# Two token-routing Mixtures of a four-layer macaron block: first choice taken from the logits, weights without shares, counts of tiles by one scan, counts of batches added on TensorE, fewer steps from rank to slot

## The chip, the cores and the metric

The kernel runs on one core of a Trainium2 chip. The metric is the device time of one execution in microseconds (us), of which several runs are taken; the median counts. The engines are TensorE (PE), VectorE (DVE), ScalarE (ACT), GpSimd (POOL) and SyncE (SP), whose queue issues most DMAs.

## The reference, cut to what matters

The input x holds 4 batches of 512 tokens of width 128, in f32. Four layers follow one another. Each is "macaron": x + half a feed-forward of norm(x), then x + attention of norm(x), then x + half the same feed-forward again. Layer 0's feed-forward is a mixture of 8 experts with one choice per token and a capacity of 320 rows per expert; layer 3's is one with two choices and a capacity of 512. Layers 1 and 2 have other forms (gated sums over all experts), which the change doesn't touch. The two mixtures, cut:

```
# layer 0: one choice
probs = softmax(tokens @ gate.T)
mask = one_hot(argmax(probs))
ranks = cumsum(mask, axis=0) - 1          # how many tokens before it chose the same expert
keep = (ranks < 320) * mask
y[t] = probs[t, e] * expert_e(row ranks[t] of e)     for kept tokens, else 0

# layer 3: two choices
scores = softmax(x @ wg)
gates, idx = top_k(scores, 2);  gates = gates / sum(gates)
m = one_hot of all first choices, then of all second choices
loc = cumsum(m, axis=0) - 1 at the chosen expert
valid = loc < 512
y[t] = sum over its two choices of gates * valid * expert(row loc)
```

An expert is relu(row @ w1 + b1) @ w2 + b2 with a middle width of 512. The cumulative sums run over all 2048 tokens, so a batch's ranks need the counts of all batches before it.

## The kernel before, in words

Tokens lie on the 128 partitions; a batch is four tiles of 128 tokens. The class `Mixture` is made four times: f00 and f01 (layer 0's two halves, k = 1) and f30 and f31 (layer 3's, k = 2). It has these parts.

`empty` and `clear` write zeros into the DRAM buffers. `tokens` (L283 to L403) routes one or two batches; it is a generator, and each `yield` gives the caller room to put other work in between. It makes the column `spare` (L303, the row past the end that a dropped token is sent to), norms (L145), transposes and the logits on PE (L322, into PSUM). The softmax (L224 to L236) takes the maximum of the logits (L227), subtracts it (L229), has ACT take exp (L230), and then sums (L233), takes the reciprocal (L234) and multiplies (L235). `route` (L205 to L216) finds the first largest of 8: maximum (L208), equality (L210), times a falling rank (L211), maximum (L213), and equality to it, which is the mask (L216). With two choices `without` (L221) takes the first one out and `route` runs again. The weights are `counts` (L339 for one choice, L346 to L349 for two). Then come the sums: `pre` holds, for every tile, how many tokens of one partition in the tiles before it chose each expert. Its first row is the running count of all earlier batches, copied in at L357, and one addition per tile follows (L359). Two matmuls make a rank of it: the masks against a strictly triangular `before` (L368), and `pre` against `ones` (L369), both summed in PSUM. From the rank DVE makes `kept` (L372), the row `at` counted from the expert's first row, or downward from its last for the second choice (L374 to L377), `slot` (L379), `keep` (L381), and with `spare` (L382, L383) the row `to` as an integer (L385). POOL copies the weights beside the normed tokens (L392) and sends each tile with an indirect DMA to its rows in DRAM (L395), one DMA for each tile and choice. At the end of the last batch PE also sums the total counts (L413), which DVE uses for the rows never written (L415, L417).

`experts` (L405) loads the sorted rows of an expert (`d_f`, on SP, L426), transposes them (`dT_f`, L442), computes h (L466) and o (L501), and scatters y back by an indirect DMA (L489). `combine` (L511) reads the results back and adds them to x.

Four places call `tokens`:

- Start: f00's four batches, two rounds apart (`skewed(choices, 2)`), in a part whose order the framework plans. Around them stand the loads of layer 0's expert weights, `prep_table` (L943: `rev` loads on SP; L948: `turned` matmuls, which make the bias table of layer 0's attention) and the first weights of that attention (L137, L140: raw_wqkvT, raw_ow0T).
- Layer 0's attention: f01's `tokens` are passed as what is done `after` each batch. That function runs in an order written by hand (`manual_schedule` for PE, DVE, ACT and POOL): `tokens` with `fine=True` goes on by one yield in each slot. The last batch's routing comes after the attention has ended, a tail with nothing beside it.
- The chain of layers 1 and 2: f30's `tokens` follow the last half feed-forward of layer 2: the first pair of batches in one call (G = 8 tiles) whose dispatch is held back by `later=4`, the second pair as two calls of one batch. Here only POOL's order is as written; the framework plans the others.
- Layer 3's attention: f31's `tokens`, as in layer 0, with a tail for the last batch.

[...] The lines that the prediction uses elsewhere: L127 and L129 are the copies from PSUM by DVE or ACT, L154 the aggregate of the norm, L157 POOL's first step of the norm, L180 transposes, L587, L672, L678 and L722 the scores, maxima and sums of layer 3's attention, L1275 and L1278 the gated products of layer 2's feed-forward (`gb_f`, `y_f`), L1307 the scan of layer 2's attention, L960 the addition of a row to x by POOL.

Of the kernel before, what the change touches and what calls it, by code (L numbers as in the profile page):

```python
# [41 lines left out]
def kernel(ctx: ExitStack, tc: tile.TileContext, a: dict, out: bass.AP):  # L42
# [25 lines left out]
    for b in range(NB):  # L68
# [13 lines left out]
    before = const([P, P], "before")  # L82
    nc.gpsimd.affine_select(
        out=before, in_=ones, pattern=[[1, P]], compare_op=ALU.is_gt, fill=0.0, base=0, channel_multiplier=-1
    )
    mhalf = const([P, 2 * NT], "mhalf")
# [118 lines left out]
    def route(pool, src, g, tag, mask=None):  # L205

        mx = pool.tile([P, g], FP, name=f"mx_{tag}", tag=f"mx_{tag}")
        nc.vector.tensor_reduce(mx, src, AX.X, ALU.max)  # L208
# [14 lines left out]

    def softmax(pool, lg, g, tag):  # L224

        mx = pool.tile([P, g], FP, name=f"smx_{tag}", tag=f"smx_{tag}")
        nc.vector.tensor_reduce(mx, lg, AX.X, ALU.max)  # L227
        pr = pool.tile([P, g, E], FP, name=f"pr_{tag}", tag=f"pr_{tag}")
        nc.vector.tensor_tensor(pr, lg, bc(mx, [P, g, E]), ALU.subtract)  # L229
        nc.scalar.activation(pr, pr, AF.Exp)  # L230
        yield
        sm = pool.tile([P, g], FP, name=f"sm_{tag}", tag=f"sm_{tag}")
        nc.vector.tensor_reduce(sm, pr, AX.X, ALU.add)  # L233
        nc.vector.reciprocal(sm, sm)  # L234
        nc.vector.tensor_tensor(pr, pr, bc(sm, [P, g, E]), ALU.mult)  # L235
        return pr  # L236
# [4 lines left out]
    class Mixture:  # L241
# [7 lines left out]
        def __init__(self, tag, cap, k):  # L249
# [9 lines left out]
            self.cum = None  # L259

# [22 lines left out]
        def tokens(self, bs, wT, on="vector", pool=None, fine=False, later=0):  # L283
# [8 lines left out]
            for n, b in zip(ns, bs):  # L292
# [8 lines left out]

            spare = pool.tile([P, k, G], FP, name=f"spare_{tag}", tag=f"spare{k}{G}")
            nc.gpsimd.tensor_scalar(  # L303
                spare, bc_mid(tok_id[:, i0 : i0 + G], [P, k, G]), float(self.rows), None, ALU.add
            )
# [28 lines left out]
            pr = yield from softmax(pool, plg[:, : G * E].rearrange("p (g e) -> p g e", e=E), G, f"r{G}")  # L334
            masks = tile("masks", [P, k, G, E])
            _, best = route(pool, pr, G, f"r0{G}", masks[:, 0])
            counts = tile("counts", [P, k, G])
            if k == 1:
                nc.vector.tensor_scalar(counts[:, 0], best, 0.5, None, ALU.mult)  # L339
            else:  # L340
                if fine:
                    yield
                rest = without(pool, pr, masks[:, 0], G, -4.0, f"r{G}")
# [6 lines left out]
            if fine:  # L350
                yield
# [1183 lines left out]
```

## Time and profile before

| what | value |
|---|---|
| runs, median (lowest to highest) | 1565.0 us (1563.73 to 1570.41), 3 runs |
| profiled execution, its own time | 1562.17 us |
| its span, first to last instruction | 1560.5 us |
| mean granted TensorE clock | 0.893 |
| busy: PE, DVE, ACT, POOL | 81%, 55%, 46%, 42% |
| PE busy in layer 0's attention with what is woven in (118 to 380 us) | 229.15 of 262 us |
| PE busy in layer 3's attention (1125 to 1433 us) | 291.09 of 308 us |
| indirect DMAs of the dispatch (L395) | 96, 983 ns each on POOL |

The span is that of one execution, taken by the hardware profiler; times on the page are us from its start, and the execution took 1.67 us more than the span. A line of the page names the source line of the kernel, the engine, the operation, the tile written and those read, with partitions and elements per partition. In a view in order of time, the number in brackets is how long the engine sat idle before the instruction, and what ended that. Shares of busy time are means over stages that have different limits.

### The profile page before, as it was taken

How to read it: one execution, taken by the hardware profiler on the slowest of the kernel's cores; microseconds unless marked ns; L12 is line 12 of the kernel's file. 1: busy time of each engine (PE TensorE's matmuls, PEld its weight loads, DVE VectorE, ACT ScalarE, POOL GpSimd, SP SyncE). 2: the span in 40 equal slices, each digit the busy share in tenths (PEclk: the TensorE clock that was granted, in tenths of full speed). 3: DMA queues.
4: the chain of work that ended last, by engine and by line, in shares of the span. 5: the costliest groups of instructions: out<-in, count | busy, mean ns of one | idle time of the engine just before them, and what ended most of it. 6: DMA issues, size and time to landing. Idle time of an engine off the chain costs nothing. (4 is left out here: it accounts for less than half of the span.)

```text
span 1560.5 us, 28691 instructions
## 1 busy us (share of the span) xinstructions
PE 1264.9 (81%) x10523; PEld 821.3 (53%) x10523; DVE 864.1 (55%) x2947; ACT 712.9 (46%) x1487; POOL 655.7 (42%) x789
## 2 busy tenths in 40 slices
PE   4777998995969688989988676718779999998394
PEld 3455676773756455766756655616533343333273
DVE  5335676773325365766556455515367787774343
ACT  1234876871443165768643322203325655564041
POOL 3455767872520176777501111273632214212253
PEclk9997999996979888999999778758979999999597
DMA  7420240002515474442033302214204000000223
GB/s 231 129 57 8 77 164 12 9 13 64 148 35 109 126 226 123 136 123 69 2 78 116 135 0 109 114 50 114 64 21 171 14 3 13 12 5 15 75 79 105
DMA packets 103092, 123.12 MB, mean 79 GB/s; under 512 B 9404, under 2 KB 74152, under 8 KB 100904
## 3 DMA queue, kind: packets, MB, share of 16 engines
q1 hardware_dynamic: 96296, 108.07, 23.2%
q0 software_dynamic: 6656, 13.22, 2.6%
q8 instruction: 84, 1.38, 0.4%
q14 instruction: 56, 0.46, 0.1%
HBM read 79.27 MB, written 41.98 MB: 78 GB/s over the span
## 5 line engine op out<-in xcount | busy, mean ns | idle before, releaser
L605 POOL TENSOR_SCALAR sc_a<-sc_a,top_a 128x128 f32<-128x128 f32 (+3 forms) x256 | 275.4, 1091 | 112.1 <-DVE top_a L604 72.2
L587 PE MATMUL s_a<-k_a,q_a 32*128 32x512 f32 (+3 forms) x1536 | 267.1, 549 | 17.9 <-DMA k_a<-fac_a 14.2
L692 ACT ACTIVATE w_a<-t_a 128x512 f32<-128x512 f32 x256 | 140.4, 595 | 119.7 <-PE t_a L587 94.8
L628 PE MATMUL t_a<-ident,sc_a 128*128 128x128 f32 x1280 | 172.3, 282 | 6.0 <-DVE top_a L608 5.6
L489 POOL DMA_INDIRECT res_f<-y_f,back_f x112 | 109.7, 980 | 141.8 <-ACT y_f L488 101.3
L587 PE MATMUL t_a<-ql_a,k_a 32*128 32x512 f32 x512 | 168.8, 643 | 0.5 <-DVE low_a__12599 L672 0.2
L628 PEld LDWEIGHTS t_a<-ident,sc_a 128*128 128x128 f32 x1280 | 145.1, 144 | 36.8 <-issue 13.8
L617 ACT ACTIVATE sc_a<-sc_a,top_a 128x128 f32<-128x128 f32 (+3 forms) x256 | 135.0, 577 | 23.8 <-DVE top_a L608 23.6
L587 PEld LDWEIGHTS s_a<-k_a,q_a 32*128 32x128 f32 x1536 | 93.7, 188 | 88.9 <-issue 43.1
L637 ACT ACTIVATE w_a<-t_a 128x256 f32<-128x256 f32 (+2 forms) x192 | 94.2, 526 | 64.2 <-PE t_a L628 63.7
L395 POOL DMA_INDIRECT disp_f<-n_f,to_f x96 | 94.3, 983 | 66.8 <-issue 58.8
L501 PE MATMUL o_f<-w_l,h_f 128*128 128x128 f32 (+1 forms) x896 | 113.0, 279 | 3.8 <-DVE o_f L483 3.3
L501 PEld LDWEIGHTS o_f<-w_l,h_f 128*128 128x128 f32 (+1 forms) x896 | 103.0, 184 | 14.7 <-DVE o_f L483 6.0
L466 PE MATMUL h_f<-dT_f,w_l 128*128 128x320 f32 (+1 forms) x256 | 107.8, 559 | 2.8 <-ACT dT_f L444 2.8
L157 POOL TENSOR_SCALAR rs_f<-mv_f 128x4 f32<-128x4 f32 (+1 forms) x23 | 6.5, 281 | 233.4 <-DVE mv_f L154 232.7
L650 PE MATMUL acc_a<-w_a,vpad 128*32 128x128 f32 x2560 | 98.4, 280 | 0.6 <-DVE top_a L604 0.6
L639 ACT COPY w_a<-t_a 128x256 f32<-128x256 f32 (+2 forms) x192 | 93.7, 528 | 6.7 <-PE t_a L628 6.5
L672 DVE TENSOR_REDUCE low_a__12599<-s_a 128x1 f32<-128x512 f32 x128 | 82.1, 685 | 26.3 <-PE t_a L587 18.5
L608 DVE CUSTOM_DVE_ANT_0 sc_a<-s_a,future 128x128 f32<-128x128 f32 (+3 forms) x128 | 62.3, 487 | 57.2 <-PE s_a L587 44.2
L672 DVE TENSOR_REDUCE low_a__12597<-s_a 128x1 f32<-128x512 f32 x128 | 81.3, 683 | 20.5 <-PE t_a L587 15.1
L608 DVE CUSTOM_DVE_ANT_0 sc_a<-s_a,table 128x128 f32<-128x128 f32 (+3 forms) x128 | 62.4, 487 | 53.0 <-PE s_a L587 52.5
L488 ACT ACTIVATE y_f<-o_f,d_f 128x128 f32<-128x128 f32 (+1 forms) x112 | 38.8, 394 | 105.9 <-DVE o_f L483 102.3
(337 smaller groups left out, 2260.8 us busy)
## 6 DMA issues: line engine op xcount, KB each, us to landing
gb_f<-rows_f SPq DMA_DIRECT2D x16, 1024.0 KB
fac_a<-fac_a_sb SPq DMA_DIRECT2D x36, 256.0 KB
disp_f<-zeros_f SPq DMA_DIRECT2D x4, 2080.0 KB
d_f<-disp_f SPq DMA_DIRECT2D x32, 260.0 KB
w_l<-in_L_ffn_w_dram SPq DMA_DIRECT2D x16, 512.0 KB
cb_f<-rows_f SPq DMA_DIRECT2D x16, 512.0 KB
q_a<-fac_a SPq DMA_DIRECT2D x32, 256.0 KB
k_a<-fac_a SPq DMA_DIRECT2D x32, 256.0 KB
```

The lines of the kernel that those rows point to most:

```text
L395: nc.gpsimd.indirect_dma_start(out=self.to[c][i0 + t][:, :], out_offset=bass.IndirectOffsetOnAxis(ap=to[:, c, t : t + 1], axis=0), in_=ns[ ...
L466: nc.tensor.matmul(ps[u][:, :cap], w1[:, e, (c + u) * P : (c + u + 1) * P], dT, start=True, stop=True)
L489: nc.gpsimd.indirect_dma_start(out=self.back[e * per + s][:, :], out_offset=bass.IndirectOffsetOnAxis(ap=back[:m, s : s + 1], axis=0), in_ ...
L501: nc.tensor.matmul(po[:m, s, :], h[:, c, s * P : s * P + m], w2[:, e, c, :], start=(c == 0), stop=(c == NC - 1),)
L587: nc.tensor.matmul(ps[:, n0:n1], q[r : r + SLOT, i * P : (i + 1) * P], k[r : r + SLOT, n0:n1], start=True, stop=True)
L605: nc.gpsimd.tensor_scalar(sc, sc, top, None, ALU.subtract)
L608: nc.vector.tensor_tensor_reduce(sc, banks[r][:, :n], more, -1.0, HUGE, ALU.add, ALU.min, top)
L617: nc.scalar.activation(sc, sc, AF.Exp, bias=top, scale=-1.0)
L628: nc.tensor.transpose(ps[:, x * n + j * P : x * n + (j + 1) * P], st["sc", u, i, r0 + x][:, j * P : (j + 1) * P], ident,)
L650: nc.tensor.matmul(st["acc", u][r * SLOT : (r + 1) * SLOT, i * P : (i + 1) * P], vpads[b % 2][:, j, g * 4 + r, :], st["w", u, i, r][:, j * ...
L672: nc.vector.tensor_reduce(st["low", u][:, i, c : c + 1], ps, AX.X, ALU.max, negate=True)
L692: nc.scalar.activation(w, ps, AF.Exp)
```

## The change

It does this, in `Mixture` and the constants that it uses:

- The first choice is found in the logits themselves, in PSUM, with the maximum that the exponent needs anyway. `softmax` is gone; exp(logit - maximum) is still computed by ACT, for the weights and for the second choice. One `yield` stands where two did.
- Shares aren't divided out. With one choice the weight is 0.5 / sum of the exponentials; with two it is 0.5 / (1 + second), and that times second, because the first exponential is 1. This is computed after the rank matmuls are issued.
- Masks, `pre` and all that follows are laid out expert by expert with the tiles inside. One `tensor_tensor_scan` sums over tiles; `goes_on` is 1 but for the first tile of each expert, where it is 0 and starts the sum anew. `pre` now includes its own tile, which is why the triangular matrix becomes `not_before` (0 or -1).
- The running count of earlier batches, `cum`, is no longer put into `pre`: a third matmul (ones against `cum`, spread over the tiles) adds it in PSUM, for every batch but the first. DVE adds the last column of `pre` to it afterwards.
- `spare` and `ends` (first or last row of each expert, less `spare`) are made once per Mixture on POOL. `at`, times `kept`, summed over experts, plus `spare` gives `to`; the sum `keep` and its product are gone.

In the program's static order of instructions DVE has 2691 rows for 2787, PE 3822 for 3807, POOL 587 for 584, SP 287 for 287. At the start SP now has the load d_f_552 ahead of the last two `rev` loads (rev_510, rev_515) and of raw_wqkvT and raw_ow0T; before, it stood behind them.

The diff, cut to its core:

```diff
@@ -79,10 +79,17 @@
         out=flip, in_=ones, pattern=[[1, P]], compare_op=ALU.is_equal, fill=0.0, base=-(P - 1), channel_multiplier=1
     )
 
-    before = const([P, P], "before")
+    not_before = const([P, P], "not_before")
     nc.gpsimd.affine_select(
-        out=before, in_=ones, pattern=[[1, P]], compare_op=ALU.is_gt, fill=0.0, base=0, channel_multiplier=-1
+        out=not_before, in_=ones, pattern=[[1, P]], compare_op=ALU.is_gt, fill=0.0, base=0, channel_multiplier=-1
     )
+    nc.gpsimd.tensor_scalar(not_before, not_before, -1.0, None, ALU.add)
+
+    goes_on = {}
+    for g in (NT, 2 * NT):
+        goes_on[g] = const([P, 2 * E * g], f"goes_on{g}")
+        nc.gpsimd.memset(goes_on[g], 1.0)
+        nc.gpsimd.memset(goes_on[g].rearrange("p (e t) -> p e t", t=g)[:, :, 0], 0.0)
     mhalf = const([P, 2 * NT], "mhalf")
     nc.gpsimd.memset(mhalf, -0.5)
     e_int = const([P, E], "e_int", I32)
@@ -202,10 +209,11 @@
         return ap.unsqueeze(1).to_broadcast(shape)
 
 
-    def route(pool, src, g, tag, mask=None):
-
-        mx = pool.tile([P, g], FP, name=f"mx_{tag}", tag=f"mx_{tag}")
-        nc.vector.tensor_reduce(mx, src, AX.X, ALU.max)
+    def route(pool, src, g, tag, mask=None, mx=None):
+
+        if mx is None:
+            mx = pool.tile([P, g], FP, name=f"mx_{tag}", tag=f"mx_{tag}")
+            nc.vector.tensor_reduce(mx, src, AX.X, ALU.max)
         eq = pool.tile([P, g, E], FP, name=f"eq_{tag}", tag=f"eq_{tag}")
         nc.vector.tensor_tensor(eq, src, bc(mx, [P, g, E]), ALU.is_equal)
         nc.vector.tensor_tensor(eq, eq, bc_mid(e_rank, [P, g, E]), ALU.mult)
@@ -220,20 +228,6 @@
         rest = pool.tile([P, g, E], FP, name=f"rest_{tag}", tag=f"rest_{tag}")
         nc.vector.scalar_tensor_tensor(rest, mask, low, src, ALU.mult, ALU.add)
         return rest
-
-    def softmax(pool, lg, g, tag):
-
-        mx = pool.tile([P, g], FP, name=f"smx_{tag}", tag=f"smx_{tag}")
-        nc.vector.tensor_reduce(mx, lg, AX.X, ALU.max)
-        pr = pool.tile([P, g, E], FP, name=f"pr_{tag}", tag=f"pr_{tag}")
-        nc.vector.tensor_tensor(pr, lg, bc(mx, [P, g, E]), ALU.subtract)
-        nc.scalar.activation(pr, pr, AF.Exp)
-        yield
-        sm = pool.tile([P, g], FP, name=f"sm_{tag}", tag=f"sm_{tag}")
-        nc.vector.tensor_reduce(sm, pr, AX.X, ALU.add)
-        nc.vector.reciprocal(sm, sm)
-        nc.vector.tensor_tensor(pr, pr, bc(sm, [P, g, E]), ALU.mult)
-        return pr
 
 
     routing = ctx.enter_context(tc.tile_pool(name="routing", bufs=2))
@@ -258,6 +252,15 @@
             self.back = dram_disjoint_views(self.res, E * self.per)
             self.cum = None
 
+            self.spare = routing.tile([P, TILES], FP, name=f"spare_{tag}", tag=f"spare{k}", bufs=1)
+            nc.gpsimd.tensor_scalar(self.spare, tok_id[:, :TILES], float(self.rows), None, ALU.add)
+
+            self.ends = routing.tile([P, k, E, TILES], FP, name=f"ends_{tag}", tag=f"ends{k}", bufs=1)
+            for c, row in enumerate((first_row[self.per], last_row)[:k]):
+                nc.gpsimd.tensor_tensor(
+                    self.ends[:, c], bc(row, [P, E, TILES]), bc_mid(self.spare, [P, E, TILES]), ALU.subtract
+                )
+
         def zeroed(self, pool, tag, bufs=None):
 
             self.z = pool.tile([P, S], FP, name=f"zeros_{self.tag}", tag=tag, bufs=bufs)
@@ -298,11 +301,6 @@
                         None,
                         ALU.add,
                     )
-
-            spare = pool.tile([P, k, G], FP, name=f"spare_{tag}", tag=f"spare{k}{G}")
-            nc.gpsimd.tensor_scalar(
-                spare, bc_mid(tok_id[:, i0 : i0 + G], [P, k, G]), float(self.rows), None, ALU.add
-            )
             yield from norms([xs[b] for b in bs], rows, tag, on, fine)
             if fine:
                 yield
@@ -331,58 +329,71 @@
                 return pool.tile(shape, dtype, name=f"{name}_{tag}", tag=f"{name}{k}{G}")
 
             yield
-            pr = yield from softmax(pool, plg[:, : G * E].rearrange("p (g e) -> p g e", e=E), G, f"r{G}")
-            masks = tile("masks", [P, k, G, E])
-            _, best = route(pool, pr, G, f"r0{G}", masks[:, 0])
-            counts = tile("counts", [P, k, G])
-            if k == 1:
-                nc.vector.tensor_scalar(counts[:, 0], best, 0.5, None, ALU.mult)
-            else:
+            lg = plg[:, : G * E].rearrange("p (g e) -> p g e", e=E)
+            mx = tile("mx", [P, G])
+            nc.vector.tensor_reduce(mx, lg, AX.X, ALU.max)
+            pr = tile("pr", [P, G, E])
+            nc.vector.tensor_tensor(pr, lg, bc(mx, [P, G, E]), ALU.subtract)
+
+            nc.scalar.activation(pr, pr, AF.Exp)
+
+            masks = tile("masks", [P, k, E, G])
+            by_tile = [masks[:, c].rearrange("p e g -> p g e") for c in range(k)]
+
+            route(pool, lg, G, f"r0{G}", by_tile[0], mx)
+            yield
+            if k == 2:
+                rest = without(pool, pr, by_tile[0], G, -4.0, f"r{G}")
+                _, second = route(pool, rest, G, f"r1{G}", by_tile[1])
                 if fine:
                     yield
-                rest = without(pool, pr, masks[:, 0], G, -4.0, f"r{G}")
-                _, second = route(pool, rest, G, f"r1{G}", masks[:, 1])
-                total = tile("total", [P, G])
-                nc.vector.tensor_tensor(total, best, second, ALU.add)
-                nc.vector.reciprocal(total, total)
-                nc.vector.scalar_tensor_tensor(counts[:, 0], best, 0.5, total, ALU.mult, ALU.mult)
-                nc.vector.scalar_tensor_tensor(counts[:, 1], second, 0.5, total, ALU.mult, ALU.mult)
-            if fine:
-                yield
-
-            pre = routing.tile([P, k, G + 1, E], FP, name=f"pre_{tag}", tag=f"pre{k}{G}")
-            if self.cum is None:
-                nc.vector.memset(pre[:, :, 0, :], 0.0)
-            else:
-                nc.vector.tensor_copy(pre[:, :, 0, :], self.cum)
-            for t in range(G):
-                nc.vector.tensor_tensor(pre[:, :, t + 1, :], pre[:, :, t, :], masks[:, :, t, :], ALU.add)
-            self.cum = pre[:, :, G, :]
+
+            pre = routing.tile([P, k, E, G], FP, name=f"pre_{tag}", tag=f"pre{k}{G}")
+            nc.vector.tensor_tensor_scan(
+                pre.rearrange("p k e g -> p (k e g)"),
+                goes_on[G][:, : k * E * G],
+                masks.rearrange("p k e g -> p (k e g)"),
+                0.0, ALU.mult, ALU.add,
+            )
             yield
             if fine:
                 yield
 
-            ps = bank(f"rank_{tag}")[:, : k * G * E].rearrange("p (k g e) -> p k g e", k=k, e=E)
+            ps = bank(f"rank_{tag}")[:, : k * E * G].rearrange("p (k e g) -> p k e g", k=k, e=E)
             for c in range(k):
-                out = ps[:, c].rearrange("p g e -> p (g e)")
-                nc.tensor.matmul(out, before, masks[:, c].rearrange("p g e -> p (g e)"), start=True, stop=False)
-                nc.tensor.matmul(out, ones, pre[:, c, :G, :].rearrange("p g e -> p (g e)"), start=False, stop=True)
+                nc.tensor.matmul(ps[:, c], not_before, masks[:, c], start=True, stop=False)
+                if self.cum is not None:
+                    nc.tensor.matmul(ps[:, c], ones, bc(self.cum[:, c], [P, E, G]), start=False, stop=False)
+                nc.tensor.matmul(ps[:, c], ones, pre[:, c], start=False, stop=True)
+            cum = routing.tile([P, k, E], FP, name=f"cum_{tag}", tag=f"cum{k}")
+            if self.cum is None:
+                nc.vector.tensor_copy(cum, pre[:, :, :, G - 1])
+            else:
+                nc.vector.tensor_tensor(cum, self.cum, pre[:, :, :, G - 1], ALU.add)
+            self.cum = cum
+
+            counts = tile("counts", [P, k, G])
+            total = tile("total", [P, G])
+            if k == 1:
+                nc.vector.tensor_reduce(total, pr, AX.X, ALU.add)
+            else:
+                nc.vector.tensor_scalar(total, second, 1.0, None, ALU.add)
+            nc.vector.reciprocal(total, total)
+            nc.vector.tensor_scalar(counts[:, 0], total, 0.5, None, ALU.mult)
+            if k == 2:
+                nc.vector.tensor_tensor(counts[:, 1], second, counts[:, 0], ALU.mult)
             yield
-            kept = tile("kept", [P, k, G, E])
+            kept = tile("kept", [P, k, E, G])
             nc.vector.scalar_tensor_tensor(kept, ps, float(self.cap), masks, ALU.is_lt, ALU.mult)
-            at = tile("at", [P, k, G, E])
-            nc.vector.tensor_tensor(at[:, 0], ps[:, 0], bc_mid(first_row[self.per], [P, G, E]), ALU.add)
+            at = tile("at", [P, k, E, G])
+            nc.vector.tensor_tensor(at[:, 0], ps[:, 0], self.ends[:, 0, :, i0 : i0 + G], ALU.add)
             if k == 2:
-                nc.vector.tensor_tensor(at[:, 1], bc_mid(last_row, [P, G, E]), ps[:, 1], ALU.subtract)
+                nc.vector.tensor_tensor(at[:, 1], self.ends[:, 1, :, i0 : i0 + G], ps[:, 1], ALU.subtract)
             nc.vector.tensor_tensor(at, at, kept, ALU.mult)
             slot = tile("slot", [P, k, G])
-            nc.vector.tensor_reduce(slot, at, AX.X, ALU.add)
-            keep = tile("keep", [P, k, G])
-            nc.vector.tensor_reduce(keep, kept, AX.X, ALU.add)
-            nc.vector.tensor_tensor(slot, slot, spare, ALU.add)
-            nc.vector.tensor_tensor(keep, keep, spare, ALU.mult)
+            nc.vector.tensor_reduce(slot, at.rearrange("p k e g -> p k g e"), AX.X, ALU.add)
             to = tile("to", [P, k, G], I32)
-            nc.vector.tensor_tensor(to, slot, keep, ALU.subtract)
+            nc.vector.tensor_tensor(to, slot, bc_mid(self.spare[:, i0 : i0 + G], [P, k, G]), ALU.add)
             yield
 
             for _ in range(later):
```

## The prediction

> **What bounds the kernel now.** I read the busy shares first, then the stages that hold a Mixture's routing, then the waits of TensorE in them, then the chain that ended last, then the order of instructions in the tails.
>
> ```profile
> PE 1264.9 (81%) x10523; PEld 821.3 (53%) x10523; DVE 864.1 (55%) x2947; ACT 712.9 (46%) x1487; POOL 655.7 (42%) x789
> ```
>
> TensorE is the busiest engine, but this is a mean. The table by stretch (us, then busy time of each engine) parts it:
>
> ```profile
> 118.00:380.00 262.00, 229.15 (x2695) 164.17 (x2695) 169.93 (x756) 170.94 (x373) 172.09 (x178) 0.92 0.14 46
> 985.00:1058.00 73.00, 30.29 (x199) 28.00 (x198) 29.16 (x146) 5.44 (x14) 36.50 (x53) 0.62 0.22 76
> 1125.00:1433.00 308.00, 291.09 (x2317) 113.42 (x2318) 222.19 (x498) 165.57 (x306) 86.23 (x134) 0.96 0.10 34
> 1433.00:1474.00 41.00, 10.08 (x54) 7.05 (x54) 10.55 (x50) 1.74 (x4) 11.57 (x18) 0.59 0.19 52
> ```
>
> The first and third stretch are the attentions of layers 0 and 3, into which batches 0 to 2 of the next Mixture are woven: PE is busy 87% and 95%. The second and fourth, and 0 to 58 us, are routing with nothing beside it: every engine waits. In the third stretch PE's own waits for VectorE are small:
>
> ```profile
> PE T_a L180 <- ACT n_a L1366: 12.6, 1, 12.6
> PE low_a L678 <- DVE low_a__12597 L672: 1.9, 1, 1.9
> PE acc_a L722 <- DVE low_a__12599 L672: 0.9, 1, 0.9
> ```
>
> With one of 0.2 us that is 3.0 us on DVE in 308, and in 118 to 353 it is 0.5 us. So a lighter DVE is worth almost nothing inside attentions; only the four bare stretches can pay. The chain through the last of them (start, duration, what):
>
> ```profile
> 1446.62 1.89 PE lg_f L322 x8
> 1453.20 4.46 issue
> 1457.66 1.11 POOL disp_f L395
> ...
> 1466.64 3.23 DMA disp_f<-n_f,to_f
> 1470.90 3.32 DMA d_f<-disp_f
> 1474.22 1.09 PE dT_f L442 x4
> ```
>
> Logits end at 1448.5, the dispatch begins at 1457.66, eight indirect DMAs at 1.265 us each follow, then the load of rows. The change touches only the 9.15 us from logits to first dispatch. DVE's order of time shows them as links:
>
> ```profile
> 1452.14 0.19 DVE L216 TENSOR_TENSOR masks_f<-eq_r,first_r 128x32 f32<-128x32 f32 x1
> ...
> 1453.00 0.84 DVE L359 TENSOR_TENSOR pre_f<-pre_f,masks_f 128x16 f32<-128x16 f32 x4
> 1455.22 0.22 DVE L372 SCALAR_TENSOR_TENSOR kept_f<-rank_f,masks_f 128x64 f32<-128x64 f32 x1 [1.38 <-PE rank_f L369]
> ...
> 1456.73 0.17 DVE L385 TENSOR_TENSOR to_f<-slot_f,keep_f 128x8 int32<-128x8 f32 x1 [0.22 <-DVE keep_f L383]
> ```
>
> Dependent instructions follow every 0.22 us [...], independent ones every 0.1.
>
> [...] 128x4 takes 0.16 us, 128x64 0.22. [...] the scan at L1307 takes 1.22 us for 128x512, a 128x512 tensor_tensor 0.69. [...] the first eight h_f records after the start's idle take 4.53 us, later ones 0.432 each (3.5 for eight). [...]
>
> **The change part by part.** *Instruction counts.* Per routing DVE loses 8 instructions for one choice, 10 to 14 for two; in the program's static order 96 DVE rows go, 15 PE rows and 3 POOL rows come. The scan of 32, 64 or 128 elements isn't in the trace: below, its share of L1307 (2.4 ns an element), above, that plus a link; so 0.15 to 0.5, I take 0.15 to 0.37 by width, against 0.77 to 1.64 for the adds of L359. The `ends` on POOL (128x128) are bounded by a small instruction (0.25) and L960's 128x512 (1.27): I take 0.4 each, one for each choice of each of the four Mixtures; they lie in POOL's idle time, at the start before off_f_0, where the next thing, n_f_2, isn't ready before 18.27. If that cover is gone, 0.4 us. Moved from every call to once, `spare` saves 0.25 on POOL, which waits there anyway.
>
> *A, start (layer 0's Mixture, 0 to 58.7).* Before, `to` of batch 1 runs at 38.04, behind L227 that waits for the logits of batch 3, and its dispatch starts at 38.95; from there POOL issues 12 DMAs in a row until 53.14, and d_f is issued at 55.84. Fewer instructions bring this `to` to about 35.0, so the train ends 2.75 us earlier and d_f can go at 53.1. But SP's order changes too: d_f_552, which waits for the whole dispatch, now stands ahead of the last two table loads (rev) and of raw_wqkvT and raw_ow0T; before, all four were issued by 51.6. Their issues take 0.4 each, so the last rev goes at 54.1; the last rev of before was issued at 47.9 and waited for until 51.23, 3.3 us, so it lands near 57. PE's order is still turned, wqkvT, ow0T, dT. Four turned records at 0.6 (2.4), then 0.8 for the weights: dT at 60.2 instead of 58.68, +1.5. The turned records warm PE, so dT and h_f win back up to 0.4+1.0 of the cold 0.96+4.53; I take 1.0. Net +0.5. Bounds: rev landing at 55.5 and all warm, -0.4; turned itself cold at up to 1.2 a record and nothing won back, +4.1.
>
> *B, tail of layer 0's attention (365 to 383).* Removed ahead of `to`: sum, reciprocal, product, second maximum and the wait for exp, 1.4 us; adds to scan 0.8; keep chain 0.2; raw 2.4. Copies wu1T (0.69) and su1T (0.28), which wait for transposes, stay in between, and one matmul is added. `to` from 372.9 to 371.3, **-1.6**; bounds -2.4 and -0.8. Dispatch, d_f (380.13) and dT (382.83) follow.
>
> *C, layer 3's first Mixture (985 to 1058).* POOL's train of 32 DMAs starts at 1009.94 because the norms of batch 3 stand ahead of it: rs_3 at 1007.35, behind the last aggregate at 1007.10, which is behind the maximum of batch 2's logits on DVE. In the new DVE order the last two aggregates of batch 2's norm stand after kept and at of the first pair, which wait for PE's rank. rs_2 so goes from 1001.10 to about 1002.35, and with it logits, maximum, rs_3 and the train: **+1.2**, bounds 0 and +1.5. The earlier `to` of the first pair buys nothing: POOL is not there yet.
>
> *D, tail of layer 3's attention (1448.5 to 1457.7).* New chain from 1448.53: maximum, first choice 5 links and one independent subtraction (exp hidden beside them) 1.2; second choice 6 links 1.33; scan 0.3: 1451.4. Then PE at the cold step of 0.44: pre of the first choice, three matmuls of the second, and the count matmul, five, 2.2, and 0.2 to land: 1453.8. DVE's new order puts the copy of that count (n_f) ahead of the weights and of kept, so they wait for it too. Weights 0.5, six steps to slots 1.0: `to` ends at 1455.3 instead of 1456.90, **-1.6**; without the copy ahead -2.3; bounds -2.4 and -0.7. Behind `to` nothing changes; the d_f load starts so much earlier.
>
> *E, matmuls added where PE is the bound.* The base of earlier batches is now its own matmul. Batches 1 and 2 run inside an attention: two of them times one choice in layer 0, times two in layer 3, 6 at 0.23 (L368 to L369 warm): **+1.4**, bounds 0 and +2. Batch 0 has none, batch 3 is counted above.
>
> Sum: +0.5 -1.6 +1.2 -1.6 +1.4 = -0.1. The profiled execution took 1562.17 us, its span 1560.5, so 1.67 around it; forecast for it 1562.1. The median of the runs is 2.8 above the profiled one: **1564.9**.
>
> **Rivals.** *Same (main case).* As worked out; own range 1560.5 to 1568.5.
>
> *Faster.* A keeps its 2.75 (rev lands while the dispatch still runs, or was never late), C costs nothing, B and D give 2.4 and 2.3, E stands: -2.75-2.4-2.3+1.4 = -6.0; with the 1.5 of DVE waits of the attentions that could go, -7.5: **1557.5**. For it: all four stretches are latency chains of DVE. Against it: the written orders of DVE and SP named above.
>
> *Slower.* One place: SP's d_f ahead of the last two table loads at the start. If turned runs cold and h_f after it as well, A is +4.1, the sum +3.5: **1568.5**. It decides from the point where the first dT starts later than about 59.3 with h_f as slow as now. For it: before, PE idles 3.2 us here and is cold after. Against: turned itself is work that warms PE.
>
> *It does not do what it says.* Were the order kept by the scheduler, nothing would move, 1565.0; the static order shows 96 DVE rows less, so hardly.
>
> **Chances.** Main 0.60, faster 0.22, slower 0.16, does nothing 0.02. A measurement of this kernel can tell about 0.5% (7.8 us) from no change. The faster case has its middle on that bound, so a bit over half of it, 0.13, and 0.01 of the main case lie beyond: 0.14. Of the slower case half, 0.08, is beyond 1572.8, and 0.01 of the main: 0.09. The rest, 0.77, is within. The range takes the main case and most of the other two: 1557.5 to 1569.5.
>
> **What would show it.** Right: dT_f of layer 0 near 60.2 with d_f issued near 53.1; `to` of the two tails 1.6 us earlier against the logits; first dispatch of layer 3's first Mixture later by about 1.2 against gb_f's last product; attentions longer by 0.5 and 0.9. Wrong: a scan of over 0.5 us, PE waiting inside an attention for pre or masks (none does now), or another engine's queue holding a woven step.

## The result and the profile after

The changed kernel took 1563.28 us (median of 22 runs, 1558.08 to 1566.84), the kernel before beside it 1566.17 (22 runs, 1562.88 to 1570.41): a ratio of 0.9979 [0.9971, 0.9987]. The same kernel measured twice more gave 1.0001 [0.9992, 1.0009] and 0.9995 [0.9982, 1.0008]. The first interval doesn't meet the second, so from one set of runs to the next 0.2% is left open: the change is worth between nothing and 3 us in 1565. All three lie within 0.5%.

The profiled execution took 1563.74 us with a span of 1562.0. That is 1.6 us more than the profiled one of before, while the medians stand level or the other way round: single executions of one kernel lie 5 us and more from their median, so stages below are compared from trace to trace, several kernels with the same stage together.

The busy shares of the page:

```profile
PE 1265.3 (81%) x10555; PEld 823.2 (53%) x10555; DVE 847.6 (54%) x2809; ACT 713.6 (46%) x1487; POOL 659.1 (42%) x789
```

DVE is busy 16.5 us less (864.1 before) with 138 instructions fewer; the time moved by a fifth of that or less. The table by stretch (us, then busy time and instructions of PE, PEld, DVE, ACT, POOL, PE's clock, DMA share, GB/s), for the same four stretches:

```profile
118.00:380.00 262.00, 230.31 (x2698) 164.58 (x2698) 167.76 (x731) 170.93 (x371) 171.40 (x176) 0.92 0.14 46
985.00:1058.00 73.00, 31.71 (x208) 29.88 (x208) 25.67 (x112) 5.45 (x14) 37.39 (x55) 0.64 0.20 75
1125.00:1433.00 308.00, 290.57 (x2328) 116.07 (x2326) 219.63 (x470) 165.38 (x304) 87.89 (x133) 0.96 0.10 35
1433.00:1474.00 41.00, 12.66 (x70) 8.37 (x70) 8.20 (x39) 3.08 (x7) 11.71 (x18) 0.65 0.17 46
```

In every stretch DVE has fewer instructions. The bare stretches (second and fourth) stay bare: no engine is busy for more than about half of them. In the third, PE's waits by name are still small:

```profile
PE T_a L187 <- ACT n_a L1377: 12.7, 1, 12.7
PE low_a L689 <- DVE low_a__12498 L683: 2.5, 2, 1.9
...
PE acc_a L733 <- DVE low_a__12500 L683: 0.6, 1, 0.6
```

With one of 0.4 and one of 0.2 that is 3.7 us on DVE, 3.0 before: by this view nothing was won there.

The chain that ended last, in the tail of layer 3's attention (start, duration, what):

```profile
1448.54 1.89 PE lg_f L320 x8
...
1453.49 0.64 PE rank_f L367 x2
1454.13 0.43 PE rank_f L364 x2
1454.55 0.43 PE rank_f L366 x2
1454.98 0.43 PE rank_f L367 x2
1455.41 0.40 PE n_f L424 x2
...
1458.32 1.11 POOL disp_f L406
...
1467.32 3.42 DMA disp_f<-n_f,to_f
...
1471.77 3.49 DMA d_f<-disp_f
1475.26 1.09 PE dT_f L453 x4
```

Logits end at 1450.43, the first dispatch begins at 1458.32: 7.9 us where there were 9.15. Not all of it arrives: from the start of the logits to the first dT it is 26.7 us where it was 27.6, because the last dispatch takes 3.42 us to land in place of 3.23 and the load of rows 3.49 in place of 3.32. Five matmuls about 0.43 apart stand in the chain one after the other (at a granted clock of 0.50 from 1453.4 to 1455.8 us; in the attention, from 1270 to 1290 us at 1.00, 0.22). The order of DVE in the same tail shows what waits for the last of them:

```profile
1453.14 0.29 DVE L352 TENSOR_TENSOR_SCAN pre_f<-goes_on,masks_f 128x64 f32<-128x64 f32 x1
...
1455.90 0.17 DVE L426 COPY n_f<-n_f 128x8 f32<-128x8 f32 x1 [1.95 <-PE n_f L424]
...
1456.28 0.22 DVE L387 SCALAR_TENSOR_TENSOR kept_f<-rank_f,masks_f 128x64 f32<-128x64 f32 x1
...
1456.98 0.26 DVE L394 TENSOR_REDUCE slot_f<-at_f 128x8 f32<-128x64 f32 x1
1457.39 0.17 DVE L396 TENSOR_TENSOR to_f<-slot_f,spare_f 128x8 int32<-128x8 f32 x1
```

The scan replaces four additions (0.84) with 0.29. Then DVE idles 1.95 us for the count matmul of L424, because its copy is ahead of `kept` in DVE's queue, though `kept` needs only the rank of L367, which is done one matmul earlier.

### The profile page after: what moved, and what is told of

Its sections match the earlier page's. It is cut to its first block, busy times and chain, and to the rows that moved or that the text cites. A ratio compares the mean times of both kernels' runs of the same rounds, so it can differ in the third digit from the quotient of the medians.

```text
span 1562.0 us, 28626 instructions
## 1 busy us (share of the span) xinstructions
PE 1265.3 (81%) x10555; PEld 823.2 (53%) x10555; DVE 847.6 (54%) x2809; ACT 713.6 (46%) x1487; POOL 659.1 (42%) x789
## 5 line engine op out<-in xcount | busy, mean ns | idle before, releaser
L598 PE MATMUL s_a<-k_a,q_a 32*128 32x512 f32 (+3 forms) x1536 | 263.8, 549 | 17.1 <-POOL k_a L1194 14.0
L648 ACT ACTIVATE w_a<-t_a 128x256 f32<-128x256 f32 (+2 forms) x192 | 94.4, 526 | 63.4 <-PE t_a L639 63.1
```

The lines of the kernel that those rows point to most:

```text
L598: nc.tensor.matmul(ps[:, n0:n1], q[r : r + SLOT, i * P : (i + 1) * P], k[r : r + SLOT, n0:n1], start=True, stop=True)
```

## The experiments

My theory: the change shortens two tails and pays that back in two places where the order of a queue changed (SP at the start, DVE in layer 3's first Mixture) and in the added matmuls. The rivals: it does nothing in any stage; or the balance hides something in the attentions, where I had put DVE at nothing.

### One Mixture at a time

Four kernels keep the old routing in three Mixtures and use the new one in the fourth (f00, f01, f30, f31). The edit, with `tokens_old` being `tokens` of before:

```diff
+NEW = ("f00",)
...
         def tokens(self, bs, wT, on="vector", pool=None, fine=False, later=0):
+            if self.tag not in NEW:
+                yield from self.tokens_old(bs, wT, on, pool, fine, later)
+                return
```

> The new routing in the first Mixture of layer 0 alone (f00, at the start); f01, f30 and f31 route as before. Forecast's step A: +0.5 us against before (bounds -0.4 and +4.1). Rival from the one pair of traces (first dT_f of layer 0 at 63.4 for 58.7 us, of which 0.7 is there from the first loads on): the load d_f on SP ahead of the last two table loads costs about +2 to +3 after the warm experts give some back. If the start were a gain after all, below -1.

Measured: 1581.01 us, 1.0012 [0.9997, 1.0026].

> The new routing in the second Mixture of layer 0 alone (f01, woven into layer 0's attention and its tail). Forecast's step B and its share of E: -1.6 + 0.5 = -1.1 us against before. Rival: the attention loses what the tail wins (one yield fewer moves the rank matmuls, and the added matmul stalls), 0 to +1. Second rival: the tail alone, -1.6 or more, since PE has slack for one matmul.

Measured: 1581.13 us, 1.0005 [0.9989, 1.0020].

> The new routing in the first Mixture of layer 3 alone (f30, behind the chain of layers 1 and 2). Forecast's step C: +1.2 us against before, because two aggregates of batch 2's norm stand behind kept and at of the first pair in DVE's order. Rival: the train of dispatches isn't what the chain waits for, or the shift is taken up, 0. A gain would be below -1.

Measured: 1583.64 us, 1.0021 [1.0010, 1.0033].

> The new routing in the last Mixture alone (f31, woven into layer 3's attention and its tail). Forecast's step D and its share of E: -1.6 + 0.9 = -0.7 us against before. Rival: DVE's relief counts inside the attention too (3 us of waits of PE for DVE in it), so that it is -2 to -3. If all four terms are as forecast their sum is -0.1; the measured whole is about -3, so at least one of the four has to lie some 2 us lower than forecast, if they add up at all.

Measured: 1576.01 us, 0.9980 [0.9970, 0.9991].

In this set of runs the kernel before took 1579.59, 14 us longer than in the other sets, so only the ratios count here. They have the expected signs for three: f30 alone costs, f31 alone gains, f00 leans to a cost (its interval still holds 1). f01 alone shows no gain in the time, though its tail is 1.7 us shorter in the trace. Their sum is +0.18%, against 0 to -0.2% for the whole: with four intervals of 0.1% each that is no contradiction, but too coarse to settle single microseconds; f30 alone costs 3.3 us by its ratio where its trace shows 1.9 at the first dispatch. What f31's gain of 3 us holds beyond its tail's 1.3 was the first hint that something in the attention itself had become shorter; its trace shows where (last experiment).

### The change again, and the load behind the tables

The changed kernel without an edit, run beside the next three:

> The changed kernel once more, beside the kernel before on this chip. If the four Mixtures alone (+1.9, +0.8, +3.3 and -3.1 us) add up, it is about +2.9 us here; if the first measurement of the whole holds on any chip, -2 to -4 us, and then the parts don't add up, because what one Mixture loses another takes back [...].

Measured: 1563.87 us, before 1564.39: 1.0001 [0.9992, 1.0009].

The next one keeps all of the change, but holds the first load of sorted rows (d_f_552) behind the load of raw_ow0T on SP, as before the change:

```diff
-        nc.sync.dma_start(raw, ap.rearrange("(k m) c -> m k c", m=m))
+        loaded[0] = nc.sync.dma_start(raw, ap.rearrange("(k m) c -> m k c", m=m))
...
-                fetch(0)
+                if self.tag == "f00":
+                    with tc.issue_after(loaded[0].ins):
+                        fetch(0)
+                else:
+                    fetch(0)
```

> The changed kernel, with the first load of sorted rows at the start (d_f_552) kept behind raw_ow0T in SP's queue, as it was before. The start's term is then the gain alone: first dT_f near 56 us in place of 63.4 and h_f cold again; against the changed kernel -2 to -4 us at the end of the start. If the queue's order were not the cause, dT_f stays near 63 and the time unchanged.

Measured: 1561.09 us, 0.9973 [0.9963, 0.9983], 0.28% (4.4 us) below the unedited kernel by the ratios, 2.8 us by the medians. SP in order of time, in the changed kernel (its queue, marked SPq):

```profile
54.24 0.36 SPq L437 DMA_DIRECT2D d_f<-disp_f  x1
54.70 0.94 SPq L954 DMA_DIRECT2D rev<-tab_rows  x2
```

The two table loads need nothing of the dispatch, but stand behind a load that waits for its last DMA (SP waited 8.9 us for the dispatch there). PE in order of time, changed kernel:

```profile
49.06 1.10 PE L959 MATMUL turned<-rev,flip 128*128 128x512 f32 x2 [0.70 <-DMA rev<-tab_rows]
59.10 3.75 PE L959 MATMUL turned<-rev,flip 128*128 128x512 f32 x4 [8.94 <-DMA rev<-tab_rows]
...
63.42 0.58 PE L453 MATMUL dT_f<-ident,d_f 128*128 128x128 f32 x3
64.64 1.61 PE L477 MATMUL h_f<-dT_f,w_l 128*128 128x320 f32 x5 [0.64 <-ACT dT_f L455]
```

And with the load behind the tables:

```profile
53.03 1.10 PE L965 MATMUL turned<-rev,flip 128*128 128x512 f32 x2 [0.20 <-DMA rev<-tab_rows]
...
58.01 0.96 PE L455 MATMUL dT_f<-ident,d_f 128*128 128x128 f32 x3 [3.15 <-DMA d_f<-disp_f]
59.60 4.55 PE L483 MATMUL h_f<-dT_f,w_l 128*128 128x320 f32 x8 [0.64 <-ACT dT_f L457]
```

Before the change:

```profile
58.68 0.96 PE L442 MATMUL dT_f<-ident,d_f 128*128 128x128 f32 x3 [3.21 <-DMA d_f<-disp_f]
60.27 4.53 PE L466 MATMUL h_f<-dT_f,w_l 128*128 128x320 f32 x8 [0.64 <-ACT dT_f L444]
```

In the changed kernel PE idles 8.94 us for `rev`, and the rows, which DVE already reads at 56.95, wait behind the tables in PE's queue. With the order kept, PE idles 3.15 us for the rows alone, as before the change. dT starts 5.4 us earlier; 2.5 of it are lost again, since dT takes 0.96 us in place of 0.58 and the first eight h_f 4.55 in place of 2.42. The kernel before shows nearly the same two times (0.96 and 4.53), at a granted clock of 0.51 from 58.6 to 64.7 us; in the changed kernel it is 1.00 from 63.4 to 64.1 and from 64.6 to 67.5. The first o_f, which has both in it, stands at 65.3 in the four kernels with the old start (64.85 to 66.14), at 67.6 in seven with the new one (66.60 to 68.43), at 64.5 in three with the order kept (64.29 to 64.74). So the order costs 3.1 us, and the shorter routing without it gains 0.8.

### Aggregates first

Two edits in orders of DVE: in f30's first pair `kept` waits in the queue until the last aggregate of batch 2's norm has been issued; in the tail the copy of n_f is issued after `to`.

```diff
+            for _ in range(2 if later else 0):
+                yield
+            if later:
+                with tc.issue_after(last_aggr[0].ins):
+                    keep()          # kept, as before
...
-            for _ in range(later):
+            for _ in range(later - 2):
...
-                    nc.vector.tensor_copy(n1, ps[:, :E])
+                    with tc.issue_after(self.sent_to.ins):
+                        nc.vector.tensor_copy(n1, ps[:, :E])
```

> The changed kernel with two edits to DVE's order: kept of the first pair in layer 3's first Mixture behind the last aggregate of batch 2's norm (as before), and in the last tail the copy of the counts (n_f) behind to_f. Forecast's step C: -1.2 us, the train of dispatches starting 5.6 us after the last product of layer 2 again in place of 6.9; step D: -0.3 to -0.7, logits to to_f 6.7 in place of 7.1. Together -1.5 to -2 us against the changed kernel. Rival: the train isn't what is waited for, 0.

Measured: 1562.67 us, 0.9987 [0.9976, 0.9997]: 0.14% (2.2 us) below the unedited kernel by the ratios, 1.2 by the medians. The two intervals overlap a little, so the time alone hardly tells them apart. Before the change the last aggregate of batch 2's norm ran well ahead of `kept` (DVE), and POOL's norm followed it:

```profile
1000.84 0.18 DVE L154 BATCH_NORM_AGGREGATE mv_f<-st_f 128x2 f32<-128x6 f32 x1
...
1004.12 0.29 DVE L372 SCALAR_TENSOR_TENSOR kept_f<-rank_f,masks_f 128x128 f32<-128x128 f32 x1 [0.55 <-PE rank_f L369]
```

```profile
1001.10 0.22 POOL L157 TENSOR_SCALAR rs_f<-mv_f 128x4 f32<-128x4 f32 x1 [26.71 <-DVE mv_f L154]
```

DVE in order of time, the unedited kernel run a third time:

```profile
1003.58 0.29 DVE L387 SCALAR_TENSOR_TENSOR kept_f<-rank_f,masks_f 128x128 f32<-128x128 f32 x1 [0.18 <-PE rank_f L367]
...
1004.05 0.24 DVE L161 BATCH_NORM_AGGREGATE mv_f<-st_f 128x2 f32<-128x6 f32 x2
```

POOL in the same execution, which waits for that aggregate to begin the norm:

```profile
1004.37 0.22 POOL L164 TENSOR_SCALAR rs_f<-mv_f 128x4 f32<-128x4 f32 x1 [28.33 <-DVE mv_f L161]
```

And DVE with the edit:

```profile
1004.77 0.30 DVE L163 BATCH_NORM_AGGREGATE mv_f<-st_f 128x2 f32<-128x6 f32 x2
1005.04 0.29 DVE L392 SCALAR_TENSOR_TENSOR kept_f<-rank_f,masks_f 128x128 f32<-128x128 f32 x1
```

The order is turned as meant, but from the start of the first pair's logits to POOL's norm of batch 2 it is 10.57 us before the change, 11.68 with it and 11.02 with the edit: two thirds of a microsecond come back of 1.1. What holds the rest was not separated; the scan and the copies of counts still stand ahead of the aggregates on DVE. In the tail, logits to `to` fell from 7.14 to 6.31 us.

### Counts added on DVE

The third matmul goes; one addition on DVE puts the count of earlier batches into `pre`:

```diff
+            own = pre
+            if self.cum is not None:
+                pre = routing.tile([P, k, E, G], FP, ...)
+                nc.vector.tensor_tensor(pre, own, bc(self.cum, [P, k, E, G]), ALU.add)
...
-                if self.cum is not None:
-                    nc.tensor.matmul(ps[:, c], ones, bc(self.cum[:, c], [P, E, G]), start=False, stop=False)
```

> The changed kernel without the added matmul: the running count of earlier batches is added to pre by one instruction on DVE, and TensorE has two matmuls per choice again. Forecast's step E: -1.4 us against the changed kernel in the attentions, and in each tail one link more on DVE for one or two matmul steps less, about even. Rival: the attentions have slack for the matmul, 0 or slightly slower by DVE's link.

Measured: 1564.48 us, 0.9992 [0.9982, 1.0003]; 0.09% below the unedited kernel by the ratios, 0.6 us above by the medians: not told from it. In the trace layer 3's attention is 0.9 us shorter and layer 0's 0.45, which is the 1.4 us that I had put on six matmuls; the time can't confirm that.

### Orders kept, and both

The changed kernel once more, beside three others:

> The changed kernel a third time, as the measure for the next three. The two measurements so far, 0.9979 and 1.0001 of the kernel before, have intervals that don't meet; a value between them (about 0.999) says that the change is worth 0 to -3 us and that chips differ by more than one interval shows; one near either says which was the odd one.

Measured: 1564.21 us, before 1564.98: 0.9995 [0.9982, 1.0008].

The edits of the two experiments on orders together:

> The changed kernel with the three edits to queue orders together: d_f_552 behind the first attention's loads on SP, kept behind the last aggregate, n_f behind to_f. If they add up (0.9973 and 0.9987 against 1.0001): 0.996 of the kernel before, some -6 us, against the changed kernel -4 to -6.

Measured: 1557.26 us (6 runs, 1555.48 to 1562.04), 0.9957 [0.9943, 0.9971]. It is the fastest of all kernels here: 0.43% less than before, 0.38% (6 us) less than the changed kernel beside it. The two intervals don't meet.

The same with the counts added on DVE:

> The same with the running count added on DVE in place of the third matmul. The traces show 0.9 and 0.45 us less in the two attentions and 0.2 each in the tails, but layer 3's first Mixture no faster: -1 to -1.5 us against e10 if that holds, [...].

Measured: 1560.43 us (5 runs), 0.9967 [0.9954, 0.9980]. The further 1 to 1.5 us that I expected didn't come. The interval overlaps that of the kernel before it, so it shows neither a gain nor a loss.

### DVE as full as before

The last one tests what the traces had suggested by then: that the attention of layer 3 is shorter because DVE has less to do there. The changed kernel gets, in f31's routing of batches 0 to 2, ten small DVE instructions more per batch. Their result isn't read by anything.

```diff
+            more = self.tag == "f31" and bs[0] < NB - 1
+            if more:
+                idle = tile("idle", [P, G, E])
+                nc.vector.tensor_copy(idle, lg)
+            def repeated(n):
+                for _ in range(n if more else 0):
+                    nc.vector.tensor_tensor(idle, idle, bc_mid(e_rank, [P, G, E]), ALU.max)
...
+            repeated(2)
...
+            repeated(4)
...
+            repeated(3)
```

> The changed kernel with ten idle small instructions on DVE (128x32 each, 0.22 us, about 2.1 us in all) in the routing of each of the first three batches of the last Mixture, at the places where the kernel before had its own; their result isn't read. New theory: in these stretches of layer 3's attention DVE is full (17.7 of 20 us before) and sets the pace though PE's waits are short, so the change's lighter DVE won about 1 us a batch: this kernel is 2 to 4 us slower than the changed one, with layer 3's attention from the first dT_f to the last logits 2 to 3 us longer. Forecast: DVE has slack in the attentions, 0.

Measured: 1567.82 us (14 runs), 1.0014 [1.0003, 1.0025], against 0.9995 [0.9982, 1.0008] for the kernel without them in the same set of runs: +0.19%, 3 us; the intervals overlap a little. From layer 3's first dT of the Mixture ahead of the attention to the last logits in its tail it took 392.50 us, without them 389.04. Of the 3.5 us, 2.5 came in steps of 1.0, 1.0 and 0.5 at the routings of batches 0, 1 and 2. The rest is not theirs: behind the attention the eight products `proj_a` took 2.07 us in this trace and 1.16 in the other. DVE in order of time, in the routing of one batch, with PE's `ot_a` (the transposes of the attention's output) ahead of it. Before the change:

```profile
1274.29 0.65 PE L741 MATMUL ot_a<-ident,ou_a 128*128 128x128 f32 x4
```

```profile
1274.90 1.28 DVE L672 TENSOR_REDUCE low_a__12599<-s_a 128x1 f32<-128x512 f32 x2
1276.14 0.07 DVE L355 MEMSET pre_f<- 128x16 f32 x1
1276.24 0.80 DVE L359 TENSOR_TENSOR pre_f<-pre_f,masks_f 128x16 f32<-128x16 f32 x4
1276.96 0.25 DVE L744 RECIPROCAL rec_a<-ot_a 128x16 f32<-128x16 f32 x1
```

After:

```profile
1277.61 0.66 PE L752 MATMUL ot_a<-ident,ou_a 128*128 128x128 f32 x4
```

```profile
1276.45 0.28 DVE L352 TENSOR_TENSOR_SCAN pre_f<-goes_on,masks_f 128x64 f32<-128x64 f32 x1
1276.65 1.26 DVE L683 TENSOR_REDUCE low_a__12500<-s_a 128x1 f32<-128x512 f32 x2
1278.31 0.26 DVE L755 RECIPROCAL rec_a<-ot_a 128x16 f32<-128x16 f32 x1 [0.39 <-PE ot_a L752]
```

And with the added instructions:

```profile
1278.72 0.66 PE L764 MATMUL ot_a<-ident,ou_a 128*128 128x128 f32 x4
```

```profile
1277.57 0.28 DVE L362 TENSOR_TENSOR_SCAN pre_f<-goes_on,masks_f 128x64 f32<-128x64 f32 x1
1277.76 0.84 DVE L347 TENSOR_TENSOR idle_f<-idle_f,e_rank 128x32 f32<-128x32 f32 x4
1278.52 1.28 DVE L695 TENSOR_REDUCE low_a__12500<-s_a 128x1 f32<-128x512 f32 x2
1279.72 0.24 DVE L767 RECIPROCAL rec_a<-ot_a 128x16 f32<-128x16 f32 x1
```

The reciprocal of `ot_a` tells who is ahead. After the change DVE arrives first and idles 0.39 us for PE. Before it, and with the added instructions, there is no bracket: DVE comes straight from its last instruction, and PE's result lies ready, for 2.02 us before the change and for 0.34 with the added instructions. The attention has 16 such reciprocals (`rec_a`). The routings of batches 0, 1 and 2 lie in three of the steps from one to the next, and the traces agree on these to a few hundredths:

| layer 3's attention | before | changed | changed, ten instructions added |
|---|---|---|---|
| PE's result lies ready for, us | 2.02, 2.08, 2.08 | 0.04 | 0.34, 0.35, 0.34 |
| DVE instructions in the step | 44 | 32 | 39 (seven of the ten fall into it) |
| the step, us | 19.55, 19.60, 19.62 | 17.80 | 18.65, 18.66, 18.66 |
| first to last reciprocal, us | 245.12 | 243.82 to 243.87 (six traces) | 246.35 |

The kernel with the new routing in f31 alone has the short steps of the changed kernel (17.80, 17.80 and 17.81), the three with the old routing in f31 the long ones (19.55 to 19.61). So it is f31's routing that sets the length of these steps. Not all of a short step is won: steps behind it get longer, and over the whole attention 1.3 us stay. With the counts added on DVE, so without the added matmuls, the two traces show 242.98 and 242.95, which is 2.1 us less than before. That adding instructions makes the steps longer is shown; that the change made them shorter by nothing but its lighter DVE is the same effect read backwards. The `yield` that went away moves work from step to step too, and wasn't tested apart.

The table by stretch for 20 us around the routing of batch 0, before:

```profile
1270.00:1290.00 20.00, 19.91 (x149) 7.36 (x149) 17.72 (x57) 10.38 (x19) 3.97 (x6) 1.00 0.03 11
```

With the added instructions:

```profile
1270.00:1290.00 20.00, 19.92 (x160) 7.29 (x160) 17.57 (x55) 10.79 (x21) 2.95 (x5) 1.00 0.01 4
```

PE shows as busy for 19.9 of 20 us in both, and DVE for 17.6 to 17.7. Without the added instructions it is 19.88 and 17.66 in one trace, 20.00 and 17.35 in another. So neither busy time tells whether PE is held up here; the order of DVE does.

## Why the total was right, step by step

The forecast was 1564.9 with a range of 1557.5 to 1569.5, and 0.77 on a change within 0.5%. The three measurements gave 1563.28, 1563.87 and 1564.21. The total holds, but two of its terms were wrong by about 2 us each, with opposite signs. That it came so close is luck: it rests on these two errors, and on a third in layer 0's attention, about balancing.

| step | forecast | measured in the traces |
|---|---|---|
| A, start | +0.5 (-0.4 to +4.1) | +2.3 |
| B, tail of layer 0's attention | -1.6 | -1.7 (logits to `to` 7.63, then 5.96) |
| C, layer 3's first Mixture | +1.2 (0 to +1.5) | +1.1 to +1.9, to the first dispatch |
| D, tail of layer 3's attention | -1.6; -2.3 without the copy ahead | -1.3; -2.1 without it |
| E, added matmuls | +1.4 | +1.35 |
| attentions, without the added matmuls | 0 | -2.1 in layer 3; +0.5 to +3.4 in layer 0, slower stretches of PE in it |

**A** had the right mechanism and the wrong size. The dispatch moved less than I took: `to` of batch 1 came at 36.34, not 35.0, and d_f was issued at 54.24, 1.6 us earlier, not 2.75. `rev` landed at 59.10, not near 57. The four `turned` records took 3.75 us, not 2.4 (1.98 before): after 8.94 us without work PE ran them at a granted clock of 0.53 (59.0 to 62.9 us; cold, in the prediction's word), while before the change it was 1.00 from 42 to 54 us; I had taken them as warm, at 0.6 each. Just behind them dT and h_f ran at 1.00; before the change, after 3.21 us without work, at 0.51. That gave back 2.5 rather than 1.0. The slower rival named this place, and the first half of its sign came true (dT later than 59.3; it came at 63.4). The second half, h_f as slow as before, didn't, so its +4.1 wasn't reached.

**B, D and E** held to 0.3 us. In D the copy of n_f ahead of `kept` cost 0.83 us where the prediction had 0.7, and the six steps from `kept` to `to` took 1.28 us, not 1.0: between the sum over experts and `to` lie 0.41, so not every dependent step is 0.22. "Behind `to` nothing changes" didn't hold quite: 0.9 of the 1.3 us reached the first dT.

**C** held, and in some traces went past its bound. POOL's norm of batch 2 came 1.1 us later in every trace of the unedited routing of f30. The first dispatch came 1.1 us later in four of them, 1.9 in three. The last aggregate of batch 3 stands behind the maximum of batch 2's logits in all, before the change too; in the three, the matmuls of these logits took 1.88 us for eight where the four show 1.06. The changed kernel run again is one of the three:

```profile
1007.23 1.88 PE L320 MATMUL lg_f<-gate,nT_f 128*128 128x8 f32 x8 [0.68 <-ACT nT_f L311]
```

**The step that failed** is the sentence "So a lighter DVE is worth almost nothing inside attentions; only the four bare stretches can pay." It was read from PE's named waits, 3.0 us in 308. In layer 3's attention, from first to last reciprocal, the change won 1.3 us with 0.9 us of added matmuls in it, and 2.1 without these, although each batch then has one more addition on DVE. Ten instructions more per batch took 2.5 us.

In layer 0's attention the same didn't happen. From first to last reciprocal it took 191.03 us before, and in nine traces with the change 192.00 to 194.88 (the added matmuls are 0.45 in seven of them). Part of that spread is PE's clock: near 195 us, eight products `s_a` take 0.71 us before and 1.24 after, four `qk_a` 1.98 and 2.51, at a granted clock of 1.00 (194.5 to 197.3 us) before and 0.69 (196.9 to 200.6 us) after. With the new routing in f01 alone it took 196.93 us, in the three kernels beside it with the old one 196.81 to 197.28. So a gain isn't seen there, and a loss isn't shown. Why the two attentions differ is open.

The terms measured sum to about 0 to +4 us, according to the trace that gives layer 0's attention; the runs say -3 to 0. Part of it is that a trace is one execution: before's, for instance, ran 32 products from 451.7 to 458.9 at a granted clock of 0.50 (groups of 2.08, 1.92 and 3.58 us that take 1.16, 1.04 and 1.95 in the traces after; the changed kernel's clock is 1.00 from 450 to 459), 3.4 us, and the changed kernel has such a stretch elsewhere, the one near 197 us. How often each falls into an execution no trace tells, so the last 2 us or so stay unplaced.

**The faster rival** (1557.5) is what the kernel does once the three orders are put back: 1557.26. Its mix was not the one I wrote down, so the agreement to the decimal is chance. The start gives 0.8 and not 2.75, C still costs 0.4 us at POOL's norm and 0.4 to 0.9 at the first dispatch, and the attention of layer 3 pays instead.

## What to carry to other kernels

When instructions are removed, look first at where the planner then puts the ones that wait: a load that waits for the last of a dispatch, set ahead of loads that are ready, took back 3.1 us, more than either tail won. A short copy whose input comes late doesn't belong ahead of a step on the path to the next transfer; here it cost 0.83 us. Where two engines were both nearly full, named waits and busy shares said nothing on which one leads. What told it was how long a finished result lay ready where they hand over: 2.0 us before the change, 0.04 after.

## What the hardware showed that I had not expected

- The scan, in one line's view (count, shortest, median and longest in ns, then the forms):

```profile
L352 DVE TENSOR_TENSOR_SCAN pre_f<-goes_on,masks_f x15: 211/225/424, 23.9 to 1453.1; 128x32 f32<-128x32 f32 x8, 128x64 f32<-128x64 f32 x6, 128x128 f32<-128x128 f32 x1
```

  By form 0.22, 0.28 and 0.42 us on the mean: from 64 to 128 elements 2.2 ns an element, where `kept` at the same widths (0.22 and 0.29) shows 1.1. At 32 elements, 0.22 us on the mean, it is as short as the other small instructions of `tokens` (128x32: 0.18 to 0.23).
- PE's lower clock at the start was worth 2.5 us: dT and the first eight h_f took 0.96 and 4.53 us at a granted clock of 0.51 before the change, 0.58 and 2.42 us at 1.00 when the tables were turned just ahead of them, so that a delay of dT by 5.4 us reached the experts as 3.1.
- Ten DVE instructions of 0.2 us in one batch's routing, in a stage in which PE is 95% busy, made that stage up to 1.0 us longer.
